# Reordering the first and the last slots of a fused attention and clustered-FFN kernel

## The chip, the cores and the metric

The kernel runs on one core of a Trainium2 chip, as one launch. The metric is the device time of that launch in microseconds. All data is float32. The engines are named as the profile names them: PE is TensorE (PEld its weight loads), DVE is VectorE, ACT is ScalarE, POOL is GpSimd, SP is SyncE, which only issues transfers here.

## The reference

Two layers with a residual each, on `x` of 8 batches x 256 tokens x 512 features:

```python
def attn(h):                      # NH, NKV, D = 32, 8, 128; G = 4
    qkv = h @ w_qkv               # 512 x 6144
    scores = einsum('bqhgd,bkhd->bhgqk', q, k) * D ** -0.5
    bias = -slopes * sqrt(max(q_pos - k_pos, 0)), -inf above the diagonal
    return (softmax(scores + bias) @ v) @ w_o

def ffn(h):                       # rows of h: 2048
    dots = softmax(h @ centroids.T / 0.1)        # 64 clusters
    hits = dots > 0.01
    query_sel, cluster_sel = any(hits, axis=1), any(hits, axis=0)
    row_sel = cluster_sel[assignments]           # 512 output columns
    return where(query_sel[:, None] & row_sel[None, :], h @ weight.T + bias, 0)

x = x + attn(layernorm(x))
x = x + ffn(layernorm(x))
```

`cluster_sel` depends on every row of the batch. So no output can be written before the logits of the last tokens are known.

## The kernel before

**Tiling.** The 2048 tokens are 16 tiles of 128. Two batches (512 tokens, four tiles) form a pair `p`; there are four pairs. A group `g` is one key/value head of one pair with its four query heads; a unit `u = 2 g + bb` is one batch of a group, 64 units in all. The loop `for u in range(NU + 2)` (L653) has one slot per unit and two more for the work that trails: in slot `u` the kernel makes the scores of unit `u`, the exponential of unit `u - 1`, and the attention product and output projection of unit `u - 2`.

**Products.** The projections of q, k, v and of the output are done by a Strassen-Winograd scheme: seven half-size products instead of eight. `strassen` (L136) returns a function `step(i)`; `k(1)`, `q(6)`, `e(2)` in the text are such steps. Sums of the inputs (S1 to S4 of the weights, T1 to T4 of the activations) are made on POOL or DVE beforehand (`a_sums` L107, `b_sums` L120). Products 1, 6, 7 and 4 accumulate in one PSUM bank, and ACT copies it out after each (L158); product 2 (bank "b") and products 5 and 3 (bank "c") are added to the result by DVE (L162, L165, L168). A next accumulation into a bank waits for the copy or add of the one before. Step 5 makes its product and adds it in one go; step 3 goes into the same bank.

**Order.** The order is written out by hand: each engine has one queue, and runs its instructions in the order in which the program's statements are made; semaphores make an engine wait for the others. The lines from L782 on are this order for a slot: even and odd units, the last unit, and the two slots behind it (L805 and L812). `e` is a v or k projection (`project_v` L316), `qq` the next group's q projection, `w` the output projection (`project_out` L455), `av` the attention product (`attend` L430), `f` the FFN of a tile of an earlier pair.

**Softmax.** `scores` (L359) makes a unit's scores in three matmuls, with the bias added by DVE (L373, L379). `over_keys` (L385) reduces over keys on DVE; `over_quadrants` (L393) transposes the result on PE (tp_r, L398), reduces it, stores the row to HBM and loads it back, broadcast to all partitions (L407, L416). `subtract_max` (L419) takes the maximum off, part on POOL (L423) and part on DVE (L426), then ACT takes the exponential (L747). All units do this in the slot after their scores; ahead of the loop (L613 to L645) the first four tiles are normalised and transposed and the first k and q projections are made.

**Tail.** The loop's last two slots make the last attention outputs, normalise tiles 12 to 15 (`norm_stats` L254, `norm_root`, `norm_scale`, `norm_write` L278), transpose them (`ffn_transpose` L506) and finish the FFN of tiles 10 and 11 (`ffn_hits` L564, `ffn_qsel`, `ffn_end` L575). After the loop (L873 on) come the logits, maxima and exponentials of tiles 12 to 15, the column selection (cnt, csel, rsel, L889 to L895), the dense products, and for every tile a masked copy (`copy_predicated`, L916 and L928) of the selected columns with its store. Tiles 0 to 7 were parked in HBM and are read back into `back`; tiles 1 to 3 (`SPLIT`) are finished on POOL (L911, L912). PSUM has eight banks: three in `p_acc`, two in `p_long` (tags "aw", "aq"), two in `p_sc`, one in `p_tp`.

The masked copies, as they stand before:

```python
    nc.vector.copy_predicated(xt, rsel.bitcast(I32).unsqueeze(1).to_broadcast([P, TPP, H]), yt)   # L916
    for n, t in enumerate((8, 9, 10, last, 11, last + 1, 0, last + 2, last + 3)):                 # L918
        if t in (last, last + 1):
            ffn_bias_add(t, y_of(i)), ffn_end(t)
        if t >= last + 2:
            nc.vector.scalar_tensor_tensor(y_of(i), y_sb[t][0], ffn_sb[t], y_of(i), ALU.mult, ALU.add)
        nc.vector.copy_predicated(xt, rsel.bitcast(I32), yt)                                      # L928
        (nc.sync if n % 2 == 0 else nc.scalar).dma_start(of[ts(t, P), :], xt)
```

Of the kernel before, what the change touches and what calls it, by code (L numbers as in the profile page):

```python
# [14 lines left out]
F32 = mybir.dt.float32  # L15
# [10 lines left out]
P = 128  # L26
# [27 lines left out]
def block_kernel(  # L54
# [81 lines left out]
    def strassen(name, tag, a, b, pairs, c, n):  # L136

        ps = {}  # L140

        def product(i, bank, first):
            mms = pairs(a[FACTORS[i][0]], b[FACTORS[i][1]])
            for j, (cols, lhsT, rhs) in enumerate(mms):
                nc.tensor.matmul(bank[:, cols], lhsT=lhsT, rhs=rhs, start=first and j == 0,  # L145
                                 stop=j == len(mms) - 1, skip_group_check=True)

        def like(bank, x):
            return bank[:, :n] if len(x.shape) == 2 else bank[:, :n].rearrange("p (e t) -> p e t", e=x.shape[1])

        def step(i):
            if i in (1, 5):
                pool, t = (p_long, tag) if i == 1 else (p_acc, "acc")
                ps[i] = pool.tile([P, 512], F32, tag=t, name=f"ps_{name}{'ac'[i == 5]}")
            if i in (1, 6, 7, 4):
                product(i, ps[1], i == 1)
                x = c[{1: 0, 6: 1, 7: 3, 4: 2}[i]]
                nc.scalar.copy(x, like(ps[1], x))  # L158
            elif i == 2:
                bank = p_acc.tile([P, 512], F32, tag="acc", name=f"ps_{name}b")  # L160
                product(2, bank, True)
                nc.vector.tensor_add(c[0], c[0], like(bank, c[0]))  # L162
            elif i == 5:
                product(5, ps[5], True)
                nc.vector.tensor_add(c[3], c[3], like(ps[5], c[3]))  # L165
            else:
                product(3, ps[5], False)
                nc.vector.tensor_add(c[1], c[1], like(ps[5], c[1]))  # L168

        return step  # L170
# [104 lines left out]
        nc.vector.scalar_tensor_tensor(shift, mv[:, :, 0], -1.0, rstd, ALU.mult, ALU.mult)  # L275
        return tiles, rstd, shift

    def norm_write(found, tags=("xn", "xn")):  # L278
        tiles, rstd, shift = found
        for j, t in enumerate(tiles):  # L280
            xn = xn_sb[t] = work.tile([P, H], F32, tag=tags[j], name=f"xn_{t}", bufs=2)
            nc.scalar.activation(xn, x2[t], AF.Identity, bias=shift[:, j : j + 1], scale=rstd[:, j : j + 1])

    def normalise(found, tags=("xn", "xn")):
        norm_write(norm_scale(norm_root(found)), tags)
# [330 lines left out]
    tp2 = p_sc.tile([P, 512], F32, tag="sc", name="tpx_2")  # L616
    for i in range(14):
        nc.tensor.matmul(tp1[:, :P], lhsT=ones, rhs=ones, start=True, stop=True)
    found01 = norm_stats(0, 1)
    normalise(found01)  # L620
    found23 = norm_stats(2, 3)
    norm_tile(0, 0)
    sum_x(0, "")
    found23 = norm_root(found23)
    norm_tile(0, 1, tp=tp1, copy=nc.vector.tensor_copy)
    norm_write(norm_scale(found23), tags=("y", "y"))
    alibi_bias(0)
    sum_weights(gp, wk, (0, 0), D, "S1")
    load_wv(0, 0, wk[0, 0]["S1"])
# [3 lines left out]
    load_wo(0)  # L633
    nc.sync.dma_start(bias_bc, ffn_bias.partition_broadcast(P))
    k, q = project_k(0, 0), project_q(0)
    k(1)
    norm_tile(0, 2, tp=tp2, copy=nc.vector.tensor_copy)
    norm_tile(0, 3)
    k(2)
    sum_x(0, "T1 T2 T3 T4")  # L640
    a_sums(gp, wq[0], "S3 S4")
    q(1), q(2), k(6), k(7), k(5), k(4), k(3)
    sum_weights(ve, wv, (0, 0), HH)
    q(6), q(7), q(5), q(4), q(3)
    a_sums(gp, wq[1], "S1 S2 S3")  # L645
    w_ffn = None
    y_late = None
# [5 lines left out]
    for u in range(NU + 2):  # L653
# [11 lines left out]
        flush_adds()  # L665
        if bb == 0 and g >= 1:
            b_sums(gp, wo[g - 1], "T2 T4")
        if 0 < u < NU:
            subtract_max(u - 1, 0)

        e, qq = nothing, nothing
        if own and slot in (0, 1, 8, 9):
            e = project_v(p, slot // 8, bb)
        elif own and slot in (3, 7, 11):
            e = project_k(p, (slot + 1) // 4)
        elif more_p and slot == 15:
            e = project_k(p + 1, 0)
# [53 lines left out]
        def max_and_old():  # L733
            scores(u, 2)
            over_keys(s_sb[u], r, 0, ALU.max)
            if old:
                subtract_max(u - 1, 1)
            if u > 0 and slot in (0, 8):
                a_sums(ve, wv[p, slot // 8], "S3 S4")
# [3 lines left out]
                sum_x(p + 1, "T3 T4")  # L743

        def exp_old():
            if old:
                nc.scalar.activation(s_sb[u - 1], s_sb[u - 1], AF.Exp)  # L747

        def sum_old():
            if old:  # L750
                over_keys(s_sb[u - 1], r, 1, ALU.add)
# [27 lines left out]
            if more_p and slot in (11, 12):  # L779
                norm_tile(p + 1, 2 * (slot - 11) + i)  # L780

        if bb == 0 and own:  # L782
            qq(1), e(1), max_and_old(), e(2), f(0), av(0), e(6), exp_old(), av(1), more_sums(), f(1), rows_max(), f(1.5), e(7), qq(2)
            if u == 4:
                onehot_of_columns(asg)
# [17 lines left out]
            w(3), w(4)  # L803
            t_old = t_ffn
        elif bb == 0:  # L805
            sum_old(), av(0), av(1), f(0), f(1), rows()
            ffn_hits(t_old), ffn_qsel(t_old), ffn_end(t_old)
            f(1.5), w(1, 5), f(2), w(6, 2, 7)
            flush_adds()
            w(3, 4), f(3)  # L810
            found = norm_root(norm_stats(last, last + 1))
        else:  # L812
            av(0), f(0), norm_write(norm_scale(found), tags=("y", "y")), av(1), f(1)
            ffn_max(t_ffn), ffn_exp(t_ffn)
            w(1, 2, 5, 6, 3)
            found = norm_root(norm_stats(last + 2))
            w(7)
            ffn_transpose(last, "bc"), ffn_transpose(last + 1, "snap")
            norm_write(norm_scale(found))
            w(4)  # L820
            normalise(norm_stats(last + 3))
            ffn_first(t_ffn, w_ffn), f(2), f(3)


        for dst, src in stores:
# [45 lines left out]


    y_of = lambda i: y_last[i // 2][:, i % 2, :]  # L873
    ffn_logits_product(last, w_ffn, p_long, "aq")
    ffn_transpose(last + 2, copy=nc.vector.tensor_copy)
    ffn_logits_product(last + 1, w_ffn)
    ffn_max(last), ffn_exp(last)
    ffn_transpose(last + 3, "o_s", tp=p_acc.tile([P, 512], F32, tag="acc", name="tpx_late"), copy=nc.vector.tensor_copy)
    ffn_max(last + 1), ffn_exp(last + 1)
    ffn_logits_product(last + 2, w_ffn), ffn_logits_product(last + 3, w_ffn)  # L880
    ffn_max(last + 2), ffn_exp(last + 2)
    ffn_hits(last)
    ffn_max(last + 3), ffn_exp(last + 3, work.tile([P, NCL], F32, tag="kT", name="e_last", bufs=2))
    ffn_dense(last, w_ffn, (0, 1))
    for i in (1, 2, 3):
        ffn_hits(last + i)


    cnt = p_tp.tile([P, 512], F32, tag="tp", name="cnt")  # L889
    nc.tensor.matmul(cnt[:NCL, :P], lhsT=hits_any, rhs=ones, start=True, stop=True)  # L890
    csel = work.tile([NCL, P], F32, tag="oT", name="csel")
    nc.vector.tensor_scalar(csel, cnt[:NCL, :P], 0.0, None, ALU.is_gt)
    ffn_dense(last + 1, w_ffn, (0,))
    rsel = p_tp.tile([P, 512], F32, tag="tp", name="rsel")
    nc.tensor.matmul(rsel, lhsT=csel, rhs=onehot, start=True, stop=True)  # L895
    ffn_dense(last, w_ffn, (2, 3))
    for i in (2, 3, 0):
        ffn_qsel(last + i)

    for i in (2, 3):  # L900
        nc.scalar.activation(y_of(i), bias_bc, AF.Copy, scale=ffn_sb[last + i])
        gp(y_of(i), y_of(i), x2[last + i], ALU.add)
    ffn_qsel(last + 1)
    ffn_dense(last + 1, w_ffn, (1, 2, 3))
    rsel_sb = work.tile([P, H], F32, tag="s", name="rsel_sb", bufs=3)
    nc.scalar.copy(rsel_sb, rsel)
    ffn_dense(last + 2, w_ffn, pool=p_long, tag="aw")
    ffn_dense(last + 3, w_ffn)
    for t in SPLIT:
        xt, yt = back[0][0][:, t, :], back[0][1][:, t, :]  # L910
        gp(yt, yt, rsel_sb, ALU.mult)  # L911
        gp(xt, xt, yt, ALU.add)  # L912
        nc.gpsimd.dma_start(of[ts(t, P), :], xt)

    xt, yt = back[1]
    nc.vector.copy_predicated(xt, rsel.bitcast(I32).unsqueeze(1).to_broadcast([P, TPP, H]), yt)  # L916
    nc.scalar.dma_start(of[PT_TOK : 2 * PT_TOK, :].rearrange("(i p) h -> p i h", p=P), xt)
    for n, t in enumerate((8, 9, 10, last, 11, last + 1, 0, last + 2, last + 3)):  # L918
        p, i = divmod(t, TPP)
        if t in (last, last + 1):  # L920
            ffn_bias_add(t, y_of(i)), ffn_end(t)
        if t >= last + 2:
            nc.vector.scalar_tensor_tensor(y_of(i), y_sb[t][0], ffn_sb[t], y_of(i), ALU.mult, ALU.add)
        if p < NPAIR - 2:
            xt, yt = back[p][0][:, i, :], back[p][1][:, i, :]
        else:
            xt, yt = x2[t], y_of(i) if t >= last else y_sb[t]
        nc.vector.copy_predicated(xt, rsel.bitcast(I32), yt)  # L928
        (nc.sync if n % 2 == 0 else nc.scalar).dma_start(of[ts(t, P), :], xt)


# [21 lines left out]
```

## Time and profile before

| what | us |
|---|---|
| median of three runs (1431.24 to 1434.04) | 1431.85 |
| the profiled execution | 1431.99 |
| its span | 1430.10 |
| first transpose of data on PE starts | 6.87 |
| scores of unit 1 start (slot 1) | 47.41 |
| scores of unit 2 start (slot 2) | 64.73 |
| slot 64 starts on PE (av) | 1368.34 |
| last `hits` of tile 15 ends | 1409.02 |
| column mask `rsel` ready, copied to SBUF by ACT | 1411.71 to 1412.29 |
| last masked copy ends, last store is issued | 1426.76, 1426.79 |

The granted TensorE clock is 0.997 over the span. The profile shows one execution; times within it are microseconds from the start of the span. Its rows give an engine, a line of the kernel, an operation with its output and inputs, a start and a duration; "idle" is how long the engine stood before the instruction, with what released it. In a table of waits the three numbers are the total, the times, and the longest wait. A float32 product appears as two records per matmul, so "x8" is four matmuls. Durations of DVE and ACT overlap the next instruction's start a little: a row of 0.73 comes every 0.66 us.

### The profile page before, as it was taken

The numbers are of one execution on the slowest core, as the hardware profiler recorded it, in microseconds if no ns is written. First come the engines' busy times: TensorE is split into PE (matmuls) and PEld (weight loads), VectorE is DVE, ScalarE is ACT, GpSimd is POOL, SyncE is SP. The second block draws the span as 40 slices with busy tenths as digits, with TensorE's granted clock in tenths as the row PEclk, the third lists the DMA queues.
The fourth block names the chain that finished last, engine by engine and source line by source line (L and its number), as shares of the span: only waits on it lengthen the run. The fifth ranks groups of instructions, "written<-read, shape, count | busy, mean of one in ns | idle before, by whom it ended". The sixth has DMA issues, their size and how long they took to land.

```text
span 1430.1 us, 16553 instructions
## 1 busy us (share of the span) xinstructions
PE 1402.7 (98%) x5859; PEld 1082.0 (76%) x5859; DVE 929.5 (65%) x1717; ACT 372.2 (26%) x650; POOL 877.8 (61%) x883
## 2 busy tenths in 40 slices
PE   8899999999999999999999999999999999999997
PEld 7677777767778787777777777777777777777674
DVE  5557656676566665668656666566766666566867
ACT  3222223412232222242223222143222212212342
POOL 6387857667465654668656466565756666466653
PEclk9999999999999999999999999999999999999999
DMA  5335333443342535324333435344314352333343
GB/s 187 97 115 177 133 111 138 151 148 112 111 166 74 177 127 169 129 104 143 126 113 142 133 119 177 130 151 148 133 61 147 133 177 87 135 111 134 114 162 118
DMA packets 86976, 190.20 MB, mean 133 GB/s; under 512 B 11600, under 2 KB 19792, under 8 KB 86896
## 3 DMA queue, kind: packets, MB, share of 16 engines
q1 hardware_dynamic: 85504, 186.15, 37.9%
q10 hardware_dynamic: 1104, 2.10, 0.4%
q8 instruction: 47, 0.77, 0.2%
q0 software_dynamic: 288, 0.92, 0.2%
q14 instruction: 33, 0.27, 0.1%
HBM read 176.03 MB, written 13.11 MB: 132 GB/s over the span
## 4 chain that ended last, share of the span: by engine, by line
PE 88%; DVE 7%; DMA 2%; issue 1%; POOL 1%; ACT 1%; SPq 0%; ACTq 0%; DVEq 0%; POOLq 0%
PE ps_qa L145 14%; PE ps_oa L469 14%; PE ps_oc L469 7%; PE sc L371 7%; PE ps_qc L145 7%; PE av L447 6%; PE ps_ka L145 4%; PE sc L377 4%; PE ps_ob L469 4%; PE ps_va L145 3%; PE ps_qb L145 3%; PE av L448 3%; PE ps_kc L145 2%; PE ps_vc L145 2%; PE ps_lg L515 2%
## 5 line engine op out<-in xcount | busy, mean ns | idle before, releaser
L423 POOL TENSOR_TENSOR s<-s,bc 128x1024 f32<-128x1024 f32 x64 | 151.2, 2362 | 151.1 <-DMA bc<-row_hbm 137.2
L501 POOL TENSOR_TENSOR x<-x,snap 128x256 f32<-128x256 f32 x189 | 135.5, 733 | 166.6 <-DVE x L489 96.1
L388 DVE TRANSPOSE_TENSOR_REDUCE r<-s 128x32 f32<-128x1024 f32 x128 | 157.9, 1234 | 5.5 <-ACT s L747 4.4
L112 POOL TENSOR_TENSOR o_s<-oT 128x256 f32<-128x256 f32 x64 | 47.6, 744 | 184.8 <-DVE oT L451 184.8
L158 ACT COPY qT<-ps_qa 128x512 f32<-128x512 f32 x128 | 74.7, 583 | 287.6 <-PE ps_qa L145 287.5
L484 ACT COPY snap<-ps_oa 128x256 f32<-128x256 f32 x189 | 70.3, 372 | 271.0 <-PE ps_oa L469 270.9
L469 PE MATMUL ps_oa<-wo,oT 128*128 128x256 f32 x512 | 132.6, 381 | 2.2 <-DVE oT L451 2.2
L747 ACT ACTIVATE s<-s 128x1536 f32<-128x1536 f32 x63 | 93.5, 1484 | 148.2 <-DVE s L426 142.3
L447 PE MATMUL av<-s,v 128*128 128x512 f32 x256 | 130.8, 592 | 0.0
L145 PE MATMUL ps_qa<-xT,wq 128*128 128x256 f32 x512 | 121.1, 379 | 0.8 <-ACT qT L158 0.8
L371 PE MATMUL sc<-qT,kT 128*128 128x512 f32 x256 | 120.3, 592 | 0.0
L145 PEld LDWEIGHTS ps_qa<-xT,wq 128*128 128x128 f32 x512 | 97.2, 190 | 27.7 <-issue 16.0
L373 DVE SCALAR_TENSOR_TENSOR s<-sc,alibi 128x512 f32<-128x512 f32 x128 | 88.0, 691 | 30.9 <-PE sc L371 30.0
L469 PEld LDWEIGHTS ps_oa<-wo,oT 128*128 128x128 f32 x512 | 91.1, 190 | 20.4 <-DVE oT L451 4.6
L379 DVE SCALAR_TENSOR_TENSOR s<-sc,alibi 128x512 f32<-128x512 f32 x64 | 44.3, 692 | 84.9 <-PE sc L377 84.9
L448 PEld LDWEIGHTS av<-s,v 128*128 128x128 f32 x256 | 48.7, 190 | 61.2 <-issue 61.2
L451 DVE TENSOR_TENSOR oT<-av,bc 128x512 f32<-128x512 f32 x128 | 84.0, 683 | 11.5 <-PE av L448 10.5
L389 DVE TRANSPOSE_TENSOR_REDUCE r<-s 128x16 f32<-128x512 f32 x128 | 85.6, 669 | 0.0
L448 PE MATMUL av<-s,v 128*128 128x256 f32 x256 | 76.2, 379 | 0.0
L489 DVE TENSOR_TENSOR x<-x,ps_ob 128x256 f32<-128x256 f32 x64 | 26.9, 421 | 74.3 <-PE ps_ob L469 74.3
L371 PEld LDWEIGHTS sc<-qT,kT 128*128 128x128 f32 x256 | 48.6, 190 | 33.8 <-issue 28.9
L391 DVE TENSOR_TENSOR r<-r 128x16 f32<-128x16 f32 x128 | 69.0, 539 | 4.4
(193 smaller groups left out, 2972.1 us busy)
## 6 DMA issues: line engine op xcount, KB each, us to landing
bc<-row_hbm SPq DMA_DIRECT2D x128, 512.0 KB, 4.9
wq<-in_w_qkv SPq DMA_DIRECT2D x32, 1024.0 KB, 7.7
wo<-in_w_o SPq DMA_DIRECT2D x32, 1024.0 KB, 7.9
alibi<-al_hbm SPq DMA_DIRECT2D x24, 512.0 KB, 8.4
wk<-in_w_qkv SPq DMA_DIRECT2D x16, 512.0 KB, 9.4
wv<-in_w_qkv SPq DMA_DIRECT2D x8, 1024.0 KB, 10.9
x<-in_x SPq DMA_DIRECT2D x16, 256.0 KB, 9.4
al_hbm<-alibi SPq DMA_DIRECT2D x8, 512.0 KB, 8.9
```

The lines of the kernel that those rows point to most:

```text
L145: nc.tensor.matmul(bank[:, cols], lhsT=lhsT, rhs=rhs, start=first and j == 0, stop=j == len(mms) - 1, skip_group_check=True)
L371: nc.tensor.matmul(sc, lhsT=kT[:, t0 : t0 + P], rhs=qT[:, hh : hh + 2, t0 : t0 + S], start=True, stop=True)
L373: nc.vector.scalar_tensor_tensor(s[:, hh * S : (hh + 2) * S], sc, D ** -0.5, bias[:, hh : hh + 2, :].rearrange("p h q -> p (h q)"), ALU.mu ...
L388: nc.vector.tensor_reduce(first, s[:, :K0].rearrange("p (j q) -> p j q", q=32), AX.X, op, apply_transpose=True)
L389: nc.vector.tensor_reduce(second, s[:, K0:].rearrange("p (j q) -> p j q", q=32), AX.X, op, apply_transpose=True)
L423: gp(k0, k0, mx, sub)
L447: nc.tensor.matmul(av, lhsT=v[:, i0, vc], rhs=pT[:, hh * S : (hh + 2) * S], start=True, stop=False)
L448: nc.tensor.matmul(av3[:, :, P:S], lhsT=v[:, i0 + 1, vc], rhs=pT[:, K0 + hh * P : K0 + (hh + 2) * P].rearrange("p (h q) -> p h q", h=2), s ...
L451: ve(oT[:, e].rearrange("p k m q -> p k (m q)"), av3, inv[:, hh : hh + 2, :], ALU.mult)
L469: nc.tensor.matmul(bank[:, :HH], lhsT=x[:, e, :], rhs=y[:, e, :], start=first and e == 0, stop=e == 1, skip_group_check=True)
L501: gp(c, c, s, ALU.add)
L747: nc.scalar.activation(s_sb[u - 1], s_sb[u - 1], AF.Exp)
```

## The change

It touches five places.

- `strassen`: a step "5p" makes product 5 alone; step 5 then only adds it, if the product was made.
- The beginning: tile 0 and tile 1 are normalised one by one, tile 1's last step by DVE; k(2) stands ahead of the transposes of tiles 2 and 3; the steps of k and q alternate, and k(3), q(5) and q(3) move into slot 0.
- Slot 0 gets an order of its own: the scores of unit 0 come right after k(4), its row maximum, subtraction and exponential are made in slot 0, and slot 1 has no exponential.
- Slots 64 and 65: the transpose of the FFN tile comes before av(1); hits, qsel and end of tiles 9, 10 and 11 each come later; the square root comes later; tile 13 is transposed into bank "aq".
- The tail: logits use banks of `p_sc` and `p_long`, four bias terms are made on DVE, the last tile's dense product is made in two halves in two banks, most masked copies read the mask from its SBUF copy, and stores go by SP and ACT in a new order.

```diff
         def step(i):
-            if i in (1, 5):
+            if i in (1, "5p") or i == 5 and 5 not in ps:
+                at = 1 if i == 1 else 5
...
+                if at == 5:
+                    product(5, ps[5], True)
...
-    found01 = norm_stats(0, 1)
-    normalise(found01)
+    found0 = norm_root(norm_stats(0))
+    found1 = norm_root(norm_stats(1))
+    norm_write(norm_scale(found0))
+    norm_write(norm_scale(found1), by_vector=True)
...
-    k(1)
+    k(1), k(2)
     norm_tile(0, 2, tp=tp2, copy=nc.vector.tensor_copy)
     norm_tile(0, 3)
-    k(2)
-    sum_x(0, "T1 T2 T3 T4")
+    sum_x(0, "T1 T2")
     a_sums(gp, wq[0], "S3 S4")
-    q(1), q(2), k(6), k(7), k(5), k(4), k(3)
-    sum_weights(ve, wv, (0, 0), HH)
-    q(6), q(7), q(5), q(4), q(3)
+    q(1), q(2)
+    sum_x(0, "T3 T4")
+
+    k("5p"), q(6), k(6), q(7), k(7), k(5), q(4), k(4)
...
-        if bb == 0 and own:
+        if u == 0:
+            k(3), max_and_old()
+            sum_weights(ve, wv, (0, 0), HH, "")
+            e = project_v(0, 0, 0)
+            q_first("5p"), e(1), e(2), q_first(5), q_first(3), rows_max()
+            a_sums(ve, wv[0, 0])
+            qq(1), e(6), qq(2), e(7), e(5), qq(6), e(4), e(3), qq(7)
+            subtract_max(0, 0), subtract_max(0, 1)
+            nc.scalar.activation(s_sb[0], s_sb[0], AF.Exp)
+        elif bb == 0 and own:
...
-            sum_old(), av(0), av(1), f(0), f(1), rows()
+            sum_old(), av(0), f(0), av(1), f(1), rows()
+            ffn_first(t_ffn, w_ffn), w(1, 5)
+            ffn_max(t_ffn), ffn_exp(t_ffn)
+            f(2), w(6)
+            flush_adds()
             ffn_hits(t_old), ffn_qsel(t_old), ffn_end(t_old)
-            f(1.5), w(1, 5), f(2), w(6, 2, 7)
+            w(2, 7)
             flush_adds()
-            w(3, 4), f(3)
-            found = norm_root(norm_stats(last, last + 1))
+            w(3, 4)
+            found = norm_stats(last, last + 1)
+            t_old = t_ffn
         else:
-            av(0), f(0), norm_write(norm_scale(found), tags=("y", "y")), av(1), f(1)
+            av(0), f(0)
+            found = norm_scale(norm_root(found))
+            av(1), norm_write(found, tags=("y", "y")), f(1)
+            ffn_hits(t_old), ffn_qsel(t_old), ffn_end(t_old)
...
-            ffn_transpose(last, "bc"), ffn_transpose(last + 1, "snap")
+            ffn_transpose(last, "bc")
+            ffn_transpose(last + 1, "snap", tp=p_long.tile([P, 512], F32, tag="aq", name="tpx_late"))
...
-    for i in (2, 3):
-        nc.scalar.activation(y_of(i), bias_bc, AF.Copy, scale=ffn_sb[last + i])
-        gp(y_of(i), y_of(i), x2[last + i], ALU.add)
...
+    ffn_end(last - 1)
+    for i in (2, 3):
         ffn_qsel(last + i)
+    for i in range(TPP):
+        nc.vector.scalar_tensor_tensor(y_of(i), bias_bc, ffn_sb[last + i], x2[last + i], ALU.mult, ALU.add)
+    ffn_dense(last, w_ffn, (2, 3)), ffn_dense(last + 1, w_ffn), ffn_dense(last + 2, w_ffn)
+    for h, (pool, tag) in enumerate(((p_acc, "acc"), (p_sc, "sc"))):
+        half = pool.tile([P, 512], F32, tag=tag, name="ps_f")
+        ffn_product(last + 3, w_ffn, h * HH, HH, half)
...
+    def choose(t, mask, xt, yt, queue, cols=slice(0, H)):
+        if t >= last:
+            for ps in y_sb[t] if len(y_sb[t]) == 1 else [y_sb[t][cols.start // HH]]:
+                nc.vector.scalar_tensor_tensor(yt[:, cols], ps, ffn_sb[t], yt[:, cols], ALU.mult, ALU.add)
+        nc.vector.copy_predicated(xt[:, cols], mask[:, cols].bitcast(I32), yt[:, cols])
+        queue.dma_start(of[ts(t, P), cols], xt[:, cols])
...
+    choose(8, rsel, x2[8], y_sb[8], sp)
+    choose(9, rsel, x2[9], y_sb[9], sp)
+    nc.scalar.copy(rsel_sb, rsel)
+    choose(10, rsel_sb, x2[10], y_sb[10], act)
+    choose(11, rsel_sb, x2[11], y_sb[11], sp)
+    choose_split(SPLIT[0], act)
...
+    nc.vector.copy_predicated(xt, rsel_sb.bitcast(I32).unsqueeze(1).to_broadcast([P, TPP, H]), yt)
+    sp.dma_start(of[PT_TOK : 2 * PT_TOK, :].rearrange("(i p) h -> p i h", p=P), xt)
+    choose(0, rsel_sb, back[0][0][:, 0, :], back[0][1][:, 0, :], act)
+    choose_split(SPLIT[1], act)
+    choose(last, rsel_sb, x2[last], y_of(0), sp)
+    choose(last + 1, rsel_sb, x2[last + 1], y_of(1), sp)
+    choose_split(SPLIT[2], act)
+    choose(last + 2, rsel_sb, x2[last + 2], y_of(2), sp)
+    choose(last + 3, rsel_sb, x2[last + 3], y_of(3), act, slice(0, HH))
+    choose(last + 3, rsel_sb, x2[last + 3], y_of(3), sp, slice(HH, H))
```

`choose_split` is the POOL path of tiles 1 to 3, unchanged but for the queue of its store.

## The prediction

> **What bounds the kernel now.** I read the page first. Its busy row and its chain of waits say that TensorE works through the span; so only TensorE's gaps, and what follows its last product, can be won. The span is 1430.10 us, its execution 1431.99 (1.89 around the span), the median 1431.85; I sum against 1431.99.
>
> ```profile
> PE 1402.7 (98%) x5859; PEld 1082.0 (76%) x5859; DVE 929.5 (65%) x1717; ACT 372.2 (26%) x650; POOL 877.8 (61%) x883
> ```
>
> Then TensorE's own waits (us, times, longest) between 5 and 66 us, the stretch of the first edit:
>
> ```profile
> PE ps_va L145 <- ACT v L158: 1.9, 2, 1.5
> PE tp_r L398 <- DVE r L391: 1.8, 2, 1.0
> PE ps_ka L145 <- DVE rstd L273: 1.0, 1, 1.0
> PE ps_qa L145 <- ACT qT L158: 0.8, 1, 0.8
> PE ps_ka L145 <- ACT kT L158: 0.5, 1, 0.5
> ```
>
> About 6 us in all. The 1.5 is slot 1: a table load (1.28) and the exponential of unit 0 (1.48) stand in ScalarE's queue ahead of a copy that TensorE needs. The same view from 1366 to 1412:
>
> ```profile
> PE ps_lg L515 <- ACT xnT_xnT L292: 2.2, 2, 1.5
> PE tpx L291 <- ACT xnT_bc L292: 1.1, 1, 1.1
> PE ps_oa L469 <- ACT snap L484: 0.9, 1, 0.9
> PE lg L515 <- DVE xnT_xnT L292: 0.8, 1, 0.8
> PE cnt L890 <- DVE hits_any L568: 0.7, 1, 0.7
> PE lg L515 <- ACT e L553: 0.6, 1, 0.6
> ```
>
> From 1412 VectorE sets the end. In the timeline (start, duration, engine, ...) it waits for ScalarE's copy of the mask, then runs without a gap to the last store:
>
> ```profile
> 1411.71 0.58 ACT L906 COPY rsel_sb<-rsel 128x512 f32<-128x512 f32 x1 [0.33 <-PE rsel L895]
> 1412.33 2.50 DVE L916 COPY_PREDICATED back_wq<-rsel,back_wq 128x2048 f32<-128x2048 int32 x1 [1.94 <-ACT rsel_sb L906]
> ...
> 1416.89 1.28 POOL L911 TENSOR_TENSOR back_xT<-back_xT,rsel_sb 128x512 f32<-128x512 f32 x1
> 1417.29 1.44 DVE L581 SCALAR_TENSOR_TENSOR y_kT<-y_kT,qsel,x 128x512 f32<-128x512 f32 x1
> ...
> 1418.25 1.62 POOL L912 TENSOR_TENSOR back_xT<-back_xT 128x512 f32<-128x512 f32 x1
> 1418.76 0.73 DVE L928 COPY_PREDICATED x<-rsel,y_kT 128x512 f32<-128x512 int32 x1
> ...
> 1426.79 0.33 SPq L929 DMA_DIRECT2D out<-x  x1
> ```
>
> The reader is to see that L581, both inputs in SBUF, takes 1.44 instead of its usual 0.75: it starts when L911 ends, and L912 starts its own work when L581 ends. L928, mask in PSUM, runs at 0.73 inside L912.
>
> **Start.** Tile 0 is normalised without waiting for tile 1's statistics, and tile 1 by VectorE (L579, the same form, 0.49). x for tile 0 is ready at about 6.3 instead of 6.67, both transposes are copied by about 8.2 instead of 9.01, and k(1) starts 0.9 earlier. k(2) moves ahead of the transposes of tiles 2 and 3; these stay bound by their loads (statistics at 6.73 as before). Then k(1) k(2), transposes, q(1) q(2), k(5) run gapless to about 15.5. Now q(6) is next, and needs S2 of wq from GpSimd, whose queue isn't moved: it ended at 16.41 and should end between 16.1 and 16.4. **So the 0.9 is eaten**: TensorE idles about 0.8. Before, k(6), k(7), k(5) covered this.
>
> **Slots 0 and 1.** From q(6) on, the same products follow. At the trace's pitch (1.73 us for a q product, 0.864 for k, v and a score matmul, 0.3 for tp_r): q 5 x 1.73, k 4 x 0.864, two units' scores 6 x 0.864, v 14 x 0.864, next q 7 x 1.73, two tp_r = 42.1 us. From 16.2 that is 58.3. Gaps that stay: v(7) of slot 1 behind its copy and tp_r of slot 1, 0.46 + 0.75 and 0.24 for a restart. New ones: q(3) needs VectorE's add of q(5), which stands in VectorE's queue behind the add of v(2), whose product ends only then: 0.4 + 0.7 + 0.3 latency = 1.4; v(6) waits 0.55 for S2 of wv, as the four wv sums (0.69 each) now stand behind the row maximum; restarts 0.3. Sum: slot 2 starts at 62.0 instead of 64.7, **2.7 us gained** (1 to 4).
>
> What leaves: the 1.5 behind the exponential, 1.0 at tp_r, 0.8 + 0.5 behind copies, with restarts. The table load and exponential lie in ScalarE's queue before slot 1's first v copy, from 46.9 to 49.7; the copy is needed at 52.3. Its input, the subtraction on GpSimd, waits for the broadcast: issued at about 36.6 (row maximum 35.3, 1.37 for the row's own DMA), 5.0 to land, 2.4 to subtract: 44.2. Behind that wait on GpSimd stand the alibi of group 1 (3.6), S4 of wq (1.3), S1 to S3 of the next wq and four wo sums, done near 58; S4 is ready at 49.1 and needed at 59. SP issues row and broadcast before the loads of wq, wk and the alibi store, which thus start 5 us earlier. All hidden. The loop between is unchanged, and every start in it follows another, so I carry the 2.7 to the end.
>
> **Last two slots.** In slot 64 the transpose goes before av(1), which covers its copy: 0.85. The snapshot copy comes before the exponential, and hits/qsel/end (1.7 us of VectorE) behind the maximum: the 0.9 wait falls to 0.3. TensorE ends the slot 1.6 earlier, and the statistics of tiles 12 and 13 end at 1384.3 instead of 1387.35. In slot 65 ScalarE's copy precedes the square root, so the logits start without the 1.5 wait; the output products start at 1387.35 instead of 1390.6. Here a rule speaks against: the Trainium skill, "ScalarE: Activation LUTs", section "What ACT_TABLE_LOAD costs", gives 2.66 us for a switch with its drain, and the load now lies on the path from that copy to the scale. This trace has 1.28 (1391.16 to 1392.45, the exponential follows at once). By the row the second oT is ready 0.15 before TensorE needs it, by the rule 1.2 after. I take the row. With a bank of its own ("aq") tile 13 no longer waits for tile 12's copy (1.1). Three accumulations now wait about 0.3 each for VectorE adds, as hits and end of tile 10 (1.6, or 2.2 beside GpSimd) stand before them. The last normalisation ends 3.9 earlier (1398.0, was 1401.9); logits, maxima, exponentials and hits follow in the same count, with tile 11's bias add, hits and end moved behind the transposes: the last hits end at 1405.1 instead of 1409.02, **3.9 gained**. rsel's product follows csel at once, where a 1 us product stood between: ready at 1407.05 instead of 1411.65, 4.6 in all.
>
> **VectorE's last stretch gives much of it back.** After csel it now does end of tile 11 (0.7), two qsel (0.35), four bias terms (0.65 each, were ScalarE's and GpSimd's for two tiles, a bias add and end for two), then two masked copies from PSUM (0.66 each): 1411.0. As built, ScalarE's copy of the mask waits for the second of these, and the third waits for the copy: 0.7 of stall, 1411.75. Left: two masked copies, the 2048 wide one (2.5), one more, three times add and copy (1.33), twice the halves (0.8): 10.1, **ending at 1421.85 if nothing disturbs it.** But GpSimd's six operations (1.27) start at 1411.75 too, and the masked copies now read the mask from SBUF beside SBUF data. The row: with the mask in PSUM no delay. The rule: the Trainium skill, "SBUF — State Buffer", section "Who interferes with whom", says that a VectorE instruction with two SBUF inputs contends with a GpSimd one that reads SBUF, and the loser blocks for the whole instruction. No masked copy of this form is in the trace; L581 with two SBUF inputs, 1.44, agrees with the rule. I take it: the copies alternate with GpSimd (0.6, 1.2, 0.55, 1.2, 2.2, 1.2, 0.55, then three of 1.2 + 0.55, the adds from PSUM beside GpSimd) and the end is 1426.1, against 1426.76. By the row it is 1421.85, by the rule 4.25 later. TensorE's last tile in halves (bank free after the first add, 3.7 later done) stays ahead of both; the two new banks cost nothing. The last store is half as large: 3.3 after the copy becomes about 3.0. GpSimd's stores move to ScalarE's queue, and all but two issue well before the end.
>
> **Sum:** 2.7 + 4.6 - 3.9 (the last stretch takes 19.05 instead of 15.1) + 0.3 = 3.65 off: 1431.99 - 3.65 = 1428.3.
>
> **Rivals.** *No lock for masked copies* (0.27): the stretch takes 14.8; 2.7 + 4.6 + 0.3 + 0.3 = 7.9, 1424.1. For it, the undisturbed 2.50 of L916 beside GpSimd; against it, that mask was in PSUM. *The front lead is lost* (0.08), as new waits in slots 0 and 1 eat it: 1431.0. *GpSimd wins every grant* (0.10), the slower side: then the copies wait behind all six operations (8.1 + 10.1 after 1411.75: 1429.95, 3.85 more), and end of tiles 9 and 10 in slots 64 and 65, both with two SBUF inputs, wait behind three flushes (2.1) and the o sums (2.9): 8.85 lost of 3.65 won, 1437. It decides from the third extra GpSimd operation on (1.27 each). Against it: L581 got its turn after one.
>
> **How the numbers follow.** About 0.2% (2.9 us) can be told from no change. Forecast 0.55, own range 1426.5 to 1430.3; three quarters of it lie beyond 2.9. Faster: 0.41 + 0.27 = 0.68; same: 0.14 + 0.08 = 0.22; slower 0.10. The range 1423.0 to 1431.3 takes in the first three cases, with the front at 1 to 4, and leaves out the slower one.
>
> **What would show it.** Slot 2's first score near 62; a wait at q(6) on GpSimd and one at q(3) on VectorE; no wait behind the exponential. Output products of slot 65 near 1384.6 in the new trace (2.7 less), the last hits near 1402.4. Masked copies with SBUF mask of 1.7 us while GpSimd runs, then 0.72. It is wrong if these copies keep 0.72, if the score comes after 63.7, or if slot 65 waits for the scale.

## The result and the profile after

The changed kernel takes 1426.18 us (median of six runs, 1423.96 to 1429.19), the kernel before 1432.51 in the same comparison (six runs, 1431.24 to 1434.04): a ratio of 0.9958, 95% interval 0.9944 to 0.9972. The profiled execution has a span of 1423.90 us and took 1425.68. The forecast had 3.65 us less than before; the span lost 6.20. The median lies in the stated range (1423.0 to 1431.3), and 0.3 below the narrower one that the prediction gave for its own case (1426.5 to 1430.3).

TensorE is still busy all through:

```profile
PE 1402.3 (98%) x5867; PEld 1082.6 (76%) x5867; DVE 933.7 (66%) x1723; ACT 370.9 (26%) x649; POOL 878.9 (62%) x878
```

TensorE's own waits between 5 and 66 us (total, times, longest):

```profile
PE ps_qc L145 <- DVE qT L167: 1.3, 1, 1.3
PE ps_ka L145 <- ACT rstd L270: 0.9, 1, 0.9
PE tp_r L403 <- DVE r L396: 0.7, 1, 0.7
PE ps_va L145 <- DVE e_t L114: 0.5, 1, 0.5
PE ps_va L145 <- ACT v L161: 0.5, 1, 0.5
```

The first line is q(3) behind VectorE's queue, the fourth v(6) behind the sums of wv: both as foretold. The 1.5 behind the exponential is gone. The second line is k(1). The view names ScalarE's rstd there, which k(1) doesn't read; it reads x, which is transposed and copied by 8.66, and its weights wk. The view of that tile has the issue of the load (at 2.6) and the time to its landing, in the kernel before and in the changed one:

```profile
L204 SPq DMA_DIRECT2D wk<-in_w_qkv x1: 433/433/433, 2.6 to 2.6; - x1
DMA to landing us min/median/max: 6.3/6.3/6.3
```

```profile
L206 SPq DMA_DIRECT2D wk<-in_w_qkv x1: 434/434/434, 2.6 to 2.6; - x1
DMA to landing us min/median/max: 6.2/6.2/6.2
```

So the weights land at 8.9 and 8.8; k(1) starts at 9.11 (before, where x is copied by 9.01) and 8.91. TensorE's waits from 1360 to 1409:

```profile
PE cnt L917 <- DVE hits_any L573: 1.7, 1, 1.7
PE rsel L923 <- DVE csel L921: 0.4, 1, 0.4
PE ps_oa L474 <- DVE x L487: 0.4, 1, 0.4
```

Of the waits of slots 64 and 65 one of 0.4 is left; TensorE now waits for the last hits. In the timeline of VectorE and GpSimd behind it (start, duration, engine, ...; x2 joins two instructions):

```profile
1405.11 1.32 DVE L941 COPY_PREDICATED x<-rsel,y_late 128x512 f32<-128x512 int32 x2
1407.08 2.42 DVE L941 COPY_PREDICATED x<-rsel_sb,y_late 128x512 f32<-128x512 int32 x2 [0.65 <-ACT rsel_sb L953]
1409.40 3.64 DVE L959 COPY_PREDICATED back_wq<-rsel_sb,back_wq 128x2048 f32<-128x2048 int32 x1
...
1414.31 1.02 DVE L941 COPY_PREDICATED x<-rsel_sb,y_kT 128x512 f32<-128x512 int32 x1
```

```profile
1407.13 1.78 POOL L946 TENSOR_TENSOR back_xT<-back_xT,rsel_sb 128x512 f32<-128x512 f32 x1 [20.37 <-ACT rsel_sb L953]
1408.99 1.60 POOL L947 TENSOR_TENSOR back_xT<-back_xT 128x512 f32<-128x512 f32 x1
1410.55 4.19 POOL L946 TENSOR_TENSOR back_xT<-back_xT,rsel_sb 128x512 f32<-128x512 f32 x1
```

With the mask in PSUM two copies take 1.32; with the mask in SBUF two take 2.42 and the wide one 3.64 instead of 2.50. GpSimd's 1.27 becomes 1.6 to 4.19. Both engines lose.

The 6.20 us of span, stage by stage, from the two profiles:

| stage | forecast | measured |
|---|---|---|
| lead at the scores of unit 2 (64.73 to 62.02) | 2.7 | 2.71 |
| more in the unchanged loop, up to slot 64 | 0 | 0.82 |
| from slot 64 to the last hits (1409.02 to 1400.75) | 3.9 | 4.74 |
| from the last hits to the mask | 0.7 | 0.61 |
| from the mask to the last masked copy (15.1 to 18.2) | -3.95 | -3.08 |
| from the last copy to the end (3.34 to 2.94) | 0.3 | 0.40 |
| sum | 3.65 | 6.20 |

These are two executions, and others of the same code differ. From unit 2 to slot 64, the same loop in every kernel here, the 14 profiled executions take 1301.15 to 1303.88. In the seven whose code is the same up to unit 2 as in the changed kernel, or differs only in the exponential's place, its scores start between 61.64 and 62.91; in the two with the old beginning at 64.73 and 65.20.

### The profile page after: what moved, and what is told of

Same layout as the page of the kernel before. It is cut to its first block, busy times and chain, and to the rows that moved or that the text cites. A ratio compares the mean times of both kernels' runs of the same rounds, so it can differ in the third digit from the quotient of the medians.

```text
span 1423.9 us, 16581 instructions
## 1 busy us (share of the span) xinstructions
PE 1402.3 (98%) x5867; PEld 1082.6 (76%) x5867; DVE 933.7 (66%) x1723; ACT 370.9 (26%) x649; POOL 878.9 (62%) x878
## 4 chain that ended last, share of the span: by engine, by line
PE 91%; DVE 6%; issue 1%; POOL 1%; ACT 0%; DMA 0%; DVEq 0%; POOLq 0%; ACTq 0%
PE ps_oa L474 15%; PE ps_qa L145 14%; PE ps_oc L474 8%; PE sc L376 7%; PE ps_qc L145 7%; PE av L452 7%; PE ps_ka L145 4%; PE sc L382 4%; PE ps_va L145 4%; PE ps_ob L474 4%; PE av L453 3%; PE ps_qb L145 3%; PE ps_vc L145 2%; PE ps_kc L145 2%; PE ps_lg L520 2%; PE ps_f L520 1%
## 5 line engine op out<-in xcount | busy, mean ns | idle before, releaser
L145 PEld LDWEIGHTS ps_qa<-xT,wq 128*128 128x128 f32 x512 | 97.0, 190 | 26.2 <-issue 14.6
L396 DVE TENSOR_TENSOR r<-r 128x16 f32<-128x16 f32 x128 | 72.5, 566 | 4.4
```

## The experiments

Times are medians; ratios are to the kernel before in the same comparison. A stage is measured inside one profile, so the spread of the start doesn't enter: "0 to 2" is from the first score of unit 0 to that of unit 2 (37.90 in the changed kernel; more than the 34.28 of before, as steps of the beginning have moved into it), "the last stretch" from 1.12 behind the start of rsel's product, when the mask is ready, to the end of the last masked copy (18.2).

### Parts alone

**The beginning alone**: the kernel before with the hunks of `strassen`, of the beginning and of slot 0.

> The kernel before with the new beginning and slot 0 alone. If the lead of the first slots is carried through the unchanged loop (theory): scores of unit 2 start at 62.0 (before 64.73), the av of slot 64 at 1364.8 to 1365.6 (before 1368.34), and the time is 2.7 to 3.5 us below the kernel before. If the lead is lost on the way (rival): 62.0 as well, but slot 64 near 1368.3 and no change in time.

Measured: 1428.62 us, ratio 0.9977 (0.9969 to 0.9984), 3.7 below the 1432.30 of before. Scores of unit 2 at 62.86, not 62.0, and slot 64 at 1365.40, as expected: the lead is 1.87 at unit 2 and 2.94 at slot 64. So it isn't lost on the way; the 1.07 between are within what executions of the loop differ by. The gain in time is a little more than the 2.7 to 3.5 expected. In this execution q(6) does wait for GpSimd, as the forecast had it for the changed kernel:

```profile
PE ps_qa L145 <- POOL wq_s L114: 0.9, 1, 0.9
```

**The last two slots alone**: the new order of slots 64 and 65, the rest as before.

```diff
-            sum_old(), av(0), av(1), f(0), f(1), rows()
+            sum_old(), av(0), f(0), av(1), f(1), rows()
+            ffn_first(t_ffn, w_ffn), w(1, 5)
+            ffn_max(t_ffn), ffn_exp(t_ffn)
...
-            av(0), f(0), norm_write(norm_scale(found), tags=("y", "y")), av(1), f(1)
+            av(0), f(0)
+            found = norm_scale(norm_root(found))
+            av(1), norm_write(found, tags=("y", "y")), f(1)
...
```

> The kernel before with the new order of slots 64 and 65 alone; tile 11's bias add, hits and end stay in slot 65, the tail is the old one. Theory (TensorE's waits in the two slots were real): from the first av of slot 64 to the first output product of slot 65 18.4 us instead of 22.1, the last hits and the mask 3 to 3.8 earlier against slot 64, and, since the old last stretch of 15.1 is unchanged, 3 to 3.8 us off the time. Rival (the gain is made by the tail's new banks and by hits behind the transposes): the output products come 3.7 earlier, but the last hits at most 1 earlier, and the time falls by at most 1.

Measured: 1429.01 us, ratio 0.9977 (0.9970 to 0.9983), 3.3 less. From slot 64's av to slot 65's output products 18.37 us, before 22.13: the waits were real. But of these 3.8 us only 2.7 are left at the last hits and 1.1 at the mask, against slot 64, and the stretch from slot 64 to the end of the span is 1.5 shorter, not 3 to 3.8. The rest of this profile's gain lies in the loop, which is the loop of before: it ran 0.47 behind at unit 2 and 1.37 ahead at slot 64. So the median agrees with the theory by luck, and the trace only in half. What took the rest back is TensorE's clock. By stretch (columns: length; busy time of PE, PEld, DVE, ACT, POOL; granted clock; share and GB/s of the transfers):

```profile
1400.00:1402.00 2.00, 1.41 (x8) 1.38 (x7) 1.00 (x6) 0.76 (x4) 0.00 (x0) 0.64 0.00 0
1402.00:1404.00 2.00, 2.00 (x5) 1.16 (x5) 1.23 (x7) 0.40 (x2) 0.00 (x0) 0.50 0.00 0
1404.00:1406.00 2.00, 2.00 (x3) 0.34 (x1) 0.80 (x5) 0.00 (x0) 0.00 (x0) 0.50 0.00 0
```

After two waits of 0.7 and 0.6 the products run at half the clock for 6.9 us. The last logits took 1.97 instead of 1.10. The old tail has two dense products ahead of cnt; they took 3.73 instead of 1.94, and VectorE waited 1.86 for cnt. The profile of before had the same two waits and a clock of 1.00 there. Whether the clock falls differs from one execution to the next, so the worth of this part alone stays open between 1.5 and 3.8.

### The last stretch: do the engines block each other?

**Mask in PSUM**, as in the kernel before, for VectorE alone:

```diff
-    choose(10, rsel_sb, x2[10], y_sb[10], act)
+    choose(10, rsel, x2[10], y_sb[10], act)
...
-    nc.vector.copy_predicated(xt, rsel_sb.bitcast(I32).unsqueeze(1).to_broadcast([P, TPP, H]), yt)
+    nc.vector.copy_predicated(xt, rsel.bitcast(I32).unsqueeze(1).to_broadcast([P, TPP, H]), yt)
```

> The changed kernel; all masked copies of VectorE read the mask in PSUM again, GpSimd goes on reading the copy in SBUF. Theory (VectorE and GpSimd block each other when both read two operands in SBUF): copies 0.66 apart, the wide one 2.5, from the mask's product to the last masked copy 14.4 to 15.0 us instead of 18.2, time 3.2 to 3.8 below the changed kernel. Rival (the copies are slowed by the stores' and loads' traffic or by GpSimd in any case): still 1.0 to 1.7 a copy, 3.6 for the wide one, 18.2 in all, no change.

**GpSimd's work left out**, so that tiles 1 to 3 are stored without their selected columns; mask still in SBUF:

```diff
-        gp(yt, yt, rsel_sb, ALU.mult)
-        gp(xt, xt, yt, ALU.add)
```

> The changed kernel without the work of GpSimd in the last stretch: tiles 1 to 3 are stored without the selected columns. The masked copies still read the mask in SBUF. Theory (it takes both engines): copies 0.66 apart, the wide one 2.5, 14.4 to 15.0 us from the mask's product to the last copy, time 3.2 to 3.8 below the changed kernel. Rival (a masked copy with all operands in SBUF is slower by itself): 1.0 a copy, 3.6 for the wide one, 18.2 as in the changed kernel.

Measured: 1422.47 us (ratio 0.9935, 0.9914 to 0.9955) and 1422.98 (0.9936, 0.9917 to 0.9955); the last stretch takes 14.9 and 14.6. The wide copy in the two timelines, mask in PSUM first:

```profile
1407.42 2.46 DVE L959 COPY_PREDICATED back_wq<-rsel,back_wq 128x2048 f32<-128x2048 int32 x1
```

```profile
1408.49 2.59 DVE L957 COPY_PREDICATED back_wq<-rsel_sb,back_wq 128x2048 f32<-128x2048 int32 x1
```

Neither the mask's place nor GpSimd's work alone costs anything; 3.64 comes only with both. Take away either, and the last stretch is 3.2 or 3.5 shorter. To the end of the span both gain 2.85, as the stores then end 0.4 and 0.7 later behind the last copy; the medians fall by 3.7 and 3.2. The rule of the Trainium skill that the prediction took ("SBUF — State Buffer", "Who interferes with whom") holds here for masked copies. Its price was put too high: 4.25 in the sum, 3.2 to 3.5 by these runs.

**The mask's copy ahead of the masked copies**, added to mask_psum:

```diff
+    nc.scalar.copy(rsel_sb, rsel)
...
     choose(8, rsel, x2[8], y_sb[8], sp)
     choose(9, rsel, x2[9], y_sb[9], sp)
-    nc.scalar.copy(rsel_sb, rsel)
```

> As mask_psum, and ScalarE's copy of the mask stands ahead of the first masked copies, so that the stall of 0.65 in the middle of VectorE's queue goes and GpSimd starts at once. Theory (block between two engines with two operands in SBUF each): GpSimd now runs beside the four bias terms, which read bias and x in SBUF; these take 1.2 to 1.9 each instead of 0.65, together 2 to 4 us more; from the mask's product to the last copy 16 to 17.5 us, 1.5 to 3 later than mask_psum. Rival (only masked copies are hit): 13.6 to 14.0, 0.65 earlier than mask_psum.

Measured: 1425.12 us (ratio 0.9944, 0.9924 to 0.9963); the last stretch takes 15.8, 0.8 longer than mask_psum's 14.9. The rival is out, and the theory holds with a smaller price than the 16 to 17.5 expected. (The median is 2.7 above mask_psum's. Between the two profiles 1.3 are lost behind the mask; the rest lies ahead of it, where the edit changes nothing: wk lands 1.1 later, and the loop takes 1.9 longer.) GpSimd starts at 1405.20, when two of the four bias terms are done, and the other two take 3.42 together instead of 1.40. The lock hits these as well, both inputs in SBUF. A stall of 0.65 was exchanged for 2.0.

**TensorE's gap ahead of cnt filled**:

```diff
-    ffn_dense(last, w_ffn, (0, 1))
+    ffn_dense(last, w_ffn)
...
-    ffn_dense(last, w_ffn, (2, 3)), ffn_dense(last + 1, w_ffn), ffn_dense(last + 2, w_ffn)
+    ffn_dense(last + 1, w_ffn), ffn_dense(last + 2, w_ffn)
```

> The changed kernel; all four dense products of tile 12 stand ahead of cnt, where TensorE waited 1.7 us for the last hits. Theory (the granted clock falls to 0.5 for some 3.5 us after that gap, and VectorE, not TensorE, sets the end): the gap ahead of cnt falls below 0.1, the clock stays at 1.00 from 1400 to the end, the dense products end 3 to 3.5 earlier, and the time from the mask's product to the last masked copy stays at 18.0 to 18.4, no change in time. Rival (TensorE's slow dense products hold VectorE back): 0.5 to 2 shorter.

Measured in one run: 1426.83 us; the gap is gone, the last stretch takes 18.9. The clock, changed kernel first:

```profile
1402.00:1404.00 2.00, 2.00 (x4) 0.76 (x3) 2.00 (x6) 0.00 (x0) 0.00 (x0) 0.69 0.00 0
1404.00:1406.00 2.00, 2.00 (x3) 0.74 (x3) 2.00 (x4) 0.00 (x0) 0.00 (x0) 0.50 0.00 0
```

```profile
1402.00:1404.00 2.00, 1.87 (x4) 0.78 (x5) 2.00 (x6) 0.00 (x0) 0.00 (x0) 1.00 0.00 0
1404.00:1406.00 2.00, 2.00 (x6) 0.90 (x5) 2.00 (x4) 0.00 (x0) 0.00 (x0) 1.00 0.00 0
```

In the changed kernel TensorE runs at half its clock for 3.4 us behind the waits of 1.7 and 0.4. In the filled one it keeps the clock there, as in best1 and best2 further on, which fill the gap too. Of the eight executions with the gap six show the fall and two (no_split, front_fix) don't. The last product of the filled kernel then waits 5.4 for VectorE to free a bank, in which the clock falls too (0.60 from 1412 to 1414). No time is won: VectorE sets this end. The last stretch was expected at 18.0 to 18.4; the 0.7 more than in the changed kernel is the turns of the lock falling otherwise: tile 0's copy took 1.77 instead of 0.71, the first half of tile 15 0.45 instead of 0.99.

### The first slots

**The exponential back in slot 1**:

```diff
         def exp_old():
-            if u > 1:
+            if u > 0:
...
             subtract_max(0, 0), subtract_max(0, 1)
-            nc.scalar.activation(s_sb[0], s_sb[0], AF.Exp)
```

> The changed kernel; the exponential of unit 0 is made in slot 1 again, all else of the new slot 0 stays. Theory (half of the lead comes from taking table load and exponential out of ScalarE's queue ahead of slot 1's v copies): TensorE waits 1.0 to 1.6 us for a v copy in slot 1 and the scores of unit 2 start at 63.0 to 63.6 instead of 62.0. Rival (the lead comes from the alternating k and q steps, the exponential was hidden anyway): 62.0 to 62.2.

Measured in one run: 1424.56 us; 0 to 2 takes 37.90, as in the changed kernel; the theory falls. (Unit 2's scores start at 61.64, as this execution starts 0.38 earlier.) ScalarE in slot 1:

```profile
53.55 1.28 ACT L754 ACT_TABLE_LOAD   x1
54.84 1.49 ACT L754 ACTIVATE s<-s 128x1536 f32<-128x1536 f32 x1
56.23 0.35 ACT L161 COPY v<-ps_va 128x256 f32<-128x256 f32 x1
```

The exponential still holds back the copy behind it, but that copy ends at 56.58, and the product that needs the bank starts at 57.14 without a wait. In the kernel before table load and exponential started at 57.04, when VectorE's subtraction was done, and the same product waited 1.48. So it isn't the place in slot 0 that took the 1.5 away; by the trace it is that the exponential's input is ready at least 2.1 us earlier against TensorE's products.

**Fewer warm-up products**:

```diff
-    for i in range(14):
+    for i in range(10):
```

> The changed kernel with 10 warm-up products instead of 14, so that the first transposes need not wait for them (they ended at 7.1). Theory (the start is bound by GpSimd's sums of wq from q(6) on): the transposes start at 6.3 to 6.5 instead of 6.95, k(1) up to 0.6 earlier, but q(6) still starts at 16.0 to 16.1, now behind a wait for GpSimd of 0.3 to 0.7; scores of unit 2 at 61.9 to 62.1. Rival (TensorE bounds the start): q(6) at 15.4 to 15.6 and the scores of unit 2 at 61.4 to 61.6.

Measured in one run: 1429.45 us, and neither holds. The transposes start at 6.52, but k(1) and k(2) run at half their pace:

```profile
9.14 2.08 PE L145 MATMUL ps_ka<-xT,wk 128*128 128x256 f32 x4 [0.67 <-ACT xT L297]
11.01 1.91 PE L145 MATMUL ps_kb<-xT,wk 128*128 128x256 f32 x4
```

These take 1.10 and 1.03 in the changed kernel. The scores of unit 0 start at 26.19, 2.1 later. (The records of the granted clock show 1.00 here; the durations tell more.) After that 0 to 2 is 37.90 again. In every execution the warm-up products start at half pace, a record every 0.21 us instead of 0.11; with fourteen of them the pace doubles somewhere between 3.7 and 6.7 us, in five of thirteen executions later than 6.0. The ten end at 5.65, before it doubled here. So ten are too few in this execution; how often, one run doesn't tell.

**VectorE's order in slot 0**:

```diff
-            q_first("5p"), e(1), e(2), q_first(5), q_first(3), rows_max()
-            a_sums(ve, wv[0, 0])
+            q_first("5p"), q_first(5), e(1), e(2)
+            a_sums(ve, wv[0, 0])
+            q_first(3), rows_max()
```

> The changed kernel; in slot 0 the add of q(5) stands ahead of that of v(2) on VectorE, and the four sums of wv ahead of the row maximum's second part. Theory (both waits of TensorE come only from VectorE's order): the wait of 1.3 at q(3) falls to 0.1 to 0.3 and that of 0.55 at v(6) goes; scores of unit 2 at 60.3 to 60.7 instead of 62.0, and 1.3 to 1.7 us off the time of the changed kernel. Rival (the waits turn up again, at tp_r or at slot 1's copies behind the exponential): 61.6 to 62.0, no change in time.

Measured: 1423.80 us (ratio 0.9940, 0.9924 to 0.9955). 0 to 2 takes 35.81, 2.1 less (1.3 to 1.7 were expected); scores of unit 2 at 59.96. The waits left between 5 and 66 us:

```profile
PE ps_ka L145 <- DMA wk<-in_w_qkv: 1.5, 1, 1.5
PE tp_r L403 <- DVE r L396: 0.7, 1, 0.7
PE ps_va L145 <- ACT v L161: 0.5, 1, 0.5
```

Both new waits of the change are gone and none takes their place. The 1.5 is the landing of wk, which differs from one execution to the next: in the eleven with the new beginning and 14 warm-up products k(1) starts between 8.56 and 9.88, each time 0.13 or 0.14 behind the landing.

### Versions that beat both kernels

**Both edits together**, VectorE's order in slot 0 and the mask in PSUM:

> The changed kernel with two single edits of before together: VectorE's order in slot 0 (2.1 between the scores of units 0 and 2) and the mask read in PSUM (3.2 from the mask to the last copy). Theory (they lie in different stretches and add up): scores of unit 0 to unit 2 in 35.8, from the mask's product to the last copy 15.0, and a time 5.0 to 5.6 below the changed kernel, 1420.6 to 1421.2. Rival (the loop between takes up an earlier start): 2 to 4 below it.

Measured: 1420.79 us (1420.09 to 1425.78), ratio 0.9931 (0.9915 to 0.9947); 0 to 2 takes 35.8, the last stretch 14.9. Each stretch is as short as with its edit alone, and the median 5.4 below the changed kernel's, as expected: they add up.

**The tail besides**: ScalarE and GpSimd make the four bias terms, the mask's copy comes first, tile 12's dense product is made ahead of cnt.

```diff
+    for i in (0, 1):
+        nc.scalar.activation(y_of(i), bias_bc, AF.Copy, scale=ffn_sb[last + i])
+        gp(y_of(i), y_of(i), x2[last + i], ALU.add)
...
-    for i in range(TPP):
-        nc.vector.scalar_tensor_tensor(y_of(i), bias_bc, ffn_sb[last + i], x2[last + i], ALU.mult, ALU.add)
...
```

> As two_fixes, and in the tail: the bias terms of tiles 12 to 15 by ScalarE and GpSimd, which stand idle there, the mask's copy ahead of the masked copies, GpSimd's six operations from then on, and tile 12's dense product whole ahead of cnt. Theory (VectorE's queue alone sets the end, its masked copies read PSUM and are not blocked): from the mask's product to the last copy 11.3 to 12.3 instead of 15.0, time 2.7 to 3.7 below two_fixes. Rival (TensorE is next: its last dense half ends no earlier, or GpSimd's ten operations hold the bias terms back): 14 to 15, at most 1 below two_fixes.

Measured: 1420.10 us (1419.65 to 1420.40), ratio 0.9915 (0.9902 to 0.9928), the lowest median here, but not clear of two_fixes (1420.09 to 1425.78). The last stretch takes 12.1, as the theory has it, but the time is only 0.7 below two_fixes, not 2.7 to 3.7: from the last copy to the end of the span it is now 4.5 us instead of 3.4, which leaves 1.6, and this profile starts 0.7 later. In its windows (last two columns: share and GB/s of the transfers):

```profile
1404.00:1406.00 2.00, 2.00 (x6) 0.82 (x5) 2.00 (x2) 0.00 (x0) 1.92 (x3) 1.00 0.77 289
...
1410.00:1412.00 2.00, 1.82 (x9) 1.27 (x7) 1.95 (x4) 0.00 (x0) 1.92 (x2) 1.00 1.05 387
1412.00:1414.00 2.00, 0.00 (x0) 0.00 (x0) 1.26 (x3) 0.00 (x0) 1.27 (x1) 1.00 1.03 380
```

VectorE is done at 1413.3 and the stores run on at some 380 GB/s. Of the cause this is no proof: two_fixes ends at this rate too, and in best1 the last store is issued 0.7 after the last copy, behind GpSimd's on ScalarE's queue, where in two_fixes it follows the copy at once.

**Smaller stores, on one queue**:

```diff
-    nc.vector.copy_predicated(xt, rsel.bitcast(I32).unsqueeze(1).to_broadcast([P, TPP, H]), yt)
-    sp.dma_start(of[PT_TOK : 2 * PT_TOK, :].rearrange("(i p) h -> p i h", p=P), xt)
+    for i in range(TPP):
+        choose(TPP + i, rsel, xt[:, i, :], yt[:, i, :], sp)
```

> As best1; the wide copy of tiles 4 to 7 (1 MB in one store) is made in four copies with a store of 256 KB each, and all stores of VectorE's tiles go by SyncE's queue, so that none waits behind GpSimd's on ScalarE's. Theory (in best1 the stores set the end: they moved 380 GB/s from 1408 to 1414 without a pause, but only 102 to 289 before, and the last was issued 0.7 after its copy): the transfers are busy above 0.9 from 1405 on, the last copy ends 12.2 to 12.5 after the mask's product, the last store lands 3.0 to 3.5 after the last copy instead of 4.5, from the mask's product to the end of the span 15.3 to 15.9 instead of 16.6, time 0.7 to 1.3 below best1. Rival (the 380 GB/s bound only the last microseconds): 16.3 to 16.6, no change.

Measured: 1422.09 us (ratio 0.9929, 0.9915 to 0.9942), 2.0 above best1. In this profile 1.7 of that lie behind the mask. The last stretch is 12.2, but the end comes 6.1 after the last copy. SyncE's waits from 1400 on:

```profile
SPq L945 <- DMA out<-back_xT: 7.5, 3, 2.8
```

Three times SyncE held its next store until an earlier one had landed, and the transfers fell to 216 to 282 GB/s from 1408 to 1414. In best1 there is one such wait, of 0.6. Best2 has 17 stores instead of 14, and more of them on SyncE's queue; which of the two makes the issue wait isn't shown. Both expectations missed this. Whether the transfers' rate is a bound for best1 stays open.

## Why the prediction was right, and where its sum was off

The sign held, the stated range held, and so did the three main mechanisms: the waits of the first slots, those of the last two, and the block between VectorE and GpSimd, which mask_psum and no_split show. Two steps were wrong (k(1)'s start and why the 1.5 leaves). Of the 2.55 us more than forecast 0.82 is the loop, which the change doesn't touch; 0.84 lies in the last two slots and 0.87 in the last stretch. The range also took in two of the rivals, so the median alone decides little.

- **Start.** "k(1) 0.9 earlier" was 0.2. The sum put the load of wk at nothing: it landed at 8.9 in the kernel before, so k(1) could not start near 8.2 however early x was ready. The warm-up products, which ended at 7.1, don't explain it: in front_fix they ended at 6.4, x was copied at 8.24, and k(1) waited for wk until 9.03. At q(6) the wait of 0.8 was below 0.2 in the profiled execution, and 0.9 in front_only, 0.7 in two_fixes, 0.9 in best1. q(6) started at 16.07, right behind S2 and near the forecast 16.2. As the forecast also had GpSimd's S2 set this start, the error at k(1) hardly enters the lead.
- **Slots 0 and 1.** 1.4 at q(3) was 1.27, v(6) 0.55 was 0.55, 0.46 and 0.75 stayed. 2.7 forecast, 2.71 measured; that it agrees so closely is luck, as the spread of unit 2's start would give anything from 1.8 to 3.6. front_fix shows that the two new waits cost 2.1 us that the change could have had besides. That the 1.5 leaves because the exponential lies ahead of slot 1's copies was the wrong reason (exp_back): by the trace the earlier subtraction, which the prediction also had, does it.
- **The loop.** "Every start in it follows another, so I carry the 2.7" left out the clock. In the profile of before TensorE's clock was 0.77 and 0.50 from 301 to 305, behind a wait of 1.3 for VectorE; in slots_only, with the same loop and a wait of 1.2 at the same place, it was 1.00. With the same loop and beginning, slots_only gained 1.8 us between unit 2 and slot 64. Over all 14 profiles the loop differs by up to 2.7. So the 0.82 is no more than executions of one loop differ by, and I don't put it down to the change.
- **Last two slots.** 3.9 forecast, 4.74 measured. The term that was off: three waits of 0.3 left for VectorE's adds, and 0.3 behind the snapshot; TensorE waits once, 0.4. In six others of the eleven executions with the new last slots and tail this wait is 0.9, and 4.2 is gained instead of 4.7; so up to 0.6 of the error is the execution's. Slot 64 gave 2.04 (forecast 1.6), up to slot 65's output products 3.77 (3.25). The table load on the path took 1.28 (1380.59), the square root followed at 1381.88, and the second oT was ready at 1383.18, just as TensorE began the products (1383.17): the row holds, not the 2.66 us of the Trainium skill ("ScalarE: Activation LUTs", "What ACT_TABLE_LOAD costs").
- **Last stretch.** Forecast 19.05, measured 18.2. Without the lock 14.8 was forecast, 14.6 and 14.9 measured. The lock was sized at 4.25 and is 3.2 to 3.5: the alternation was assumed for every copy until GpSimd was done, while tile 0's copy and all adds from PSUM ran free. The stall of 0.7 was 0.65.

The rival without a lock named 1424.1, and the median, 1426.18, lies halfway between that and the forecast 1428.3. The trace decides: copies of 1.0 to 1.2 beside GpSimd and 0.73 without it. The rival in which GpSimd wins every grant fell: GpSimd was held up itself, 4.19 for 1.27.

## What to carry to other kernels

Before a mask or a factor is copied from PSUM to SBUF "for all", ask which engine reads it beside whom: VectorE reading one operand from PSUM ran free beside GpSimd here, and with all in SBUF both lost. When a start is to be moved ahead, look at all that it waits for: k(1) stood 0.2 behind a load that the table of waits didn't name. When a step is moved ahead, look whether its place or the readiness of its input was the gain, by putting the step alone back. And follow a shorter last stretch to the stores: of 2.8 us that VectorE gave (14.9 to 12.1), 1.2 came back behind its last copy.

## What the runs showed of the hardware

- TensorE's clock fell to 0.50 behind short waits: 1.7 and 0.4 in the changed kernel, 0.7 and 0.6 in slots_only, 1.3 in the loop of before. The fall lasted 3.4 us, in slots_only 6.9. In other executions the same waits left it at 1.00 (no_split and front_fix; before; slots_only). The Trainium skill ("TensorE: Matmul & The Clock Gate", "What's actually happening") has the clock fall after an idle window of about 3.4 us that runs on its own; none of these waits was longer than 1.7.
- Ten warm-up products instead of fourteen left the first data products at half pace until about 12.7 us, and the scores of unit 0 came 2.1 us later (one run). With fourteen, TensorE reached full pace 2.7 to 5.7 us after its first product, differently in each execution.
- A store can wait for the landing of an earlier one before it is issued (best2: 7.5 us in three waits; the cause isn't shown).
